# An earlier branch in the opening of a graph network and mixture-of-experts kernel, and means that are formed two slots later

## The chip, the cores and the metric

The kernel runs on one core of a Trainium2 chip. The metric is the device time in microseconds (us) of one execution, as the median of several runs. The engines are named as the profile names them: PE is TensorE (matrix products, with PEld its weight loads), DVE is VectorE, ACT is ScalarE, POOL is GpSimd, and SP is SyncE, which only starts transfers. A "q" behind an engine's name (DVEq) is that engine's sequencer, which fetches, waits and branches.

## The reference

There are 6250 nodes with 256 features and 100,000 edges with 96 features. Each edge belongs to the node whose number stands in `dst`, and `dst` is sorted. The computation, cut to what matters:

```python
h    = layernorm(x)
out1 = segment_sum(edge_attr, dst)          # 96 sums per node
cnt  = segment_sum(ones, dst)
out2 = where(cnt > 0, segment_max(edge_attr, dst), 0)
out3 = out1 / maximum(cnt, 1)               # the means
m    = concatenate([h, out1, out2, out3, u[0]])
x1   = x + h + relu(m @ W1 + b1) @ W2 + b2  # 608 -> 1024 -> 256
n    = layernorm(x1)
y    = n + (top 2 of 16 experts of n, weighted by a softmax)
out  = x1 + layernorm(y) * gamma + beta
```

## The kernel before

**Groups.** The nodes lie in 50 columns of 125 (`P`), and the columns in groups of up to four, taken from the highest node numbers down. Group 0 has two columns and group 1 has four. High nodes have few edges each, so groups 0 and 1 (`GW = 2`) are summed from *windows*: for each node the last 20 edges (`WE`) that end at its last edge are fetched and those of other nodes are masked out. All later groups take their sums and maxima from a stream over all edges, which runs on DVE beside the rest (`edge_stream`) and writes running sums to DRAM (`rows_d`).

**The opening.** Before any window can be fetched the kernel has to know where each node's edges lie. `block_starts` (L442 to L447) takes the first id of each block of 250 ids. `find_block` (ACT, L476) counts, for one column of nodes, how many blocks begin below each node. `take_blocks` turns this into a block number (DVE, L480 to L482) and fetches that block of ids for each of the 125 nodes (POOL, L485, an indirect transfer per column). `find_edge` (ACT, L492) counts in the block. `bounds` (DVE L502 and L503, PE L506 and L507) makes the place of each node's first and last edge. `index_windows` (DVE, L536 to L545) makes the window's address `win_i` and the mask `mk`, and `take_window` (POOL, L550) fetches the window, 125 x 1920 values per column.

**The check and the branch.** `check_order` (DVE, L258 to L260) and `check_fit` (DVE L266 to L268, PE L270, DVE L272 to L275) test that the ids are sorted and fit the layout, and leave a flag `misfit`. Every engine reads the flag (L1262) and branches (L1263): a body behind `tc.If`, which sums edges one by one, is run where the ids don't fit. With the given ids it isn't run, and each engine jumps over it.

**Statistics.** `stats_x` (DVE, L676 and L677), `root_x` (ACT, L682), `scale_x` (DVE, L688 to L690) and `norm_x` (ACT, L696) are the layer norm of a group's node features. `global_part` (PE L1212, DVE L1213) makes the part of the hidden layer's bias that comes from `u`. `loads_3` starts three small loads on SP.

**Windows.** For each column a window is cut twice over in two halves: `cut_window` (ACT, L558, ten rows of edges each) multiplies by the mask, for group 0 partly by DVE (L561); `sum_window` (PE, L581) adds the cut rows; `max_window` (DVE, L592, L571, L572) takes the masked maximum in the window's own buffer, so it has to wait until both cuts of the window are made; `add_window` and `mask_window` (DVE, L588 and L598) finish the sums; `mean_window` (ACT, L603 and L604) scales them to the means. Then `turn` transposes 128 features of a group at a time (PE L745, copied by ACT L746), `hidden` is the first layer (PE L756 and L761, ACT L763), and `output` the second (PE L769).

**What sets the order.** There are two stretches written by hand, ahead of the branch and behind it, each under `tc.manual_schedule()`. The second one ends with a planner: `at_slot(T, fn, ..., cost)` puts a step into a list with a due slot `T`; the list is sorted by slot and, within a slot, by the order of entry, and is then issued in that order. A group has twelve slots (`SLOTS`); a `cost` says how much DVE time a step takes from what the slot leaves for the edge stream. `mean_window` has no cost. Each engine runs its own list in order. The builder that turns this text into a program may carry single instructions ahead: in the program of before, the subtraction of `counts(0)` (L513), which the text has behind the branch, stands ahead of it on DVE, between L538 and L539.

Of the kernel before, what the change touches and what calls it, by code (L numbers as in the profile page):

```python
# [9 lines left out]
F32 = mybir.dt.float32  # L10
# [9 lines left out]
P = 125  # L20
PA = 80
RR = 8
GW = 2
# [4 lines left out]
JS = 3  # L28
# [6 lines left out]
SLOTS = 12  # L35
# [7 lines left out]
def kernel(  # L43
# [20 lines left out]
    E, EF = edge.shape  # L64
# [376 lines left out]
    def block_starts():  # L441
        nc.vector.tensor_copy(dsf, ids100[:, 0:E // 100].rearrange("p (q k) -> p q k", k=KB)[:, :, 0])  # L442
        nc.vector.tensor_tensor(dsx, ident[:100, None, :100].to_broadcast([100, QB, 100]),
                                dsf[:, :, None].to_broadcast([100, QB, 100]), op=OP.mult)
        ps_b = eps.tile([P, NBK], F32, name="ps")
        nc.tensor.matmul(ps_b, ones[:100, :P], dsx.rearrange("p q k -> p (q k)"), start=True, stop=True)
        nc.scalar.copy(b1r, ps_b)  # L447
# [22 lines left out]
    def node_cols(b):  # L470
        g0 = sum(IB[:b])
        return GRP[g0 + IB[b] - 1][0], GRP[g0][1]

    def find_block(t):
        junk = ix.tile([P, NBK], BF16, name="junk")
        nc.scalar.activation(junk, b1r, AF.Sign, scale=-1.0, bias=nhalf[:, t:t + 1], accum_out=acc1[:, t:t + 1])  # L476

    def take_blocks(a, z):
        cols = slice(a, z)
        nc.vector.tensor_scalar(blk_f[:, cols], acc1[:, cols], float(NBK), 0.5, op0=OP.add, op1=OP.mult)  # L480
        nc.vector.tensor_scalar(blk_f[:, cols], blk_f[:, cols], -1.0, 0.0, op0=OP.add, op1=OP.max)
        nc.vector.tensor_copy(blk_i[:, cols], blk_f[:, cols])  # L482
        for t in reversed(range(a, z)):
            gbs_[t] = ix.tile([P, KB], I32, name="gb", bufs=6)
            nc.gpsimd.indirect_dma_start(out=gbs_[t], out_offset=None, in_=dst_b,  # L485
                                         in_offset=IndirectOffsetOnAxis(ap=blk_i[:, t:t + 1], axis=0))
# [591 lines left out]
    def at_slot(T, fn, *a, cost=0.0):  # L1078
        tasks.append((T, len(tasks), fn, a, cost))
# [21 lines left out]
    for g, (a, z) in enumerate(GRP):  # L1101
        B, n = SLOTS * g, z - a
        if g:
            if g > 1:
                at_slot(max(0, B - 20), take_x, g)
                at_slot(B - 14, stats_x, g, 0, cost=1.2)
                at_slot(B - 13, stats_x, g, 1, cost=1.2)
            if g > 1:
                at_slot(B - 11, root_x, g)
                at_slot(B - 10, scale_x, g, cost=0.5)  # L1110
            at_slot(B - 9, norm_x, g)
            for i in range(n):
                if g >= GW:
                    late = 3 if g == GW else 0
                    at_slot(B - 10 + late + i // 2, take_edges, region[g], g, i)
                    at_slot(B - 9 + late + i // 2, take_carry, region[g], g, i)
                else:
                    for h in range(2):
                        at_slot(2 * i + h, cut_window, g, i, h * WE // 2, (h + 1) * WE // 2, None)
                        at_slot(2 * i + 1 + h, sum_half, g, i, h)  # L1120
                    at_slot(2 * i + 1, max_window, g, i, cost=4.7)
                    at_slot(2 * i + 2, add_window, g, i, cost=0.9)
                    at_slot(2 * i + 2, mask_window, g, i, cost=0.4)
                    at_slot(2 * i + 3, mean_window, g, i)
            at_slot(B - 7, keep_x, g)
            for k in range(DC):
                at_slot(B - 6 + k, turn, g, k)
            for i in range(n if g >= GW else 0):
                at_slot(B - (4 if g == GW else 6) + i // 2, join_edges, g, i, cost=0.6)
                at_slot(B - (4 if g == GW else 5) + i // 2, mask_edges, g, i)  # L1130
            for k in range(DC, KC + 1):
                at_slot(B - 3 + k - DC + (1 if g == GW and k < DC + 2 else 0), turn, g, k)
        for i in range(n):
            at_slot(B + HC + 1 + i, residual, g, i, cost=1.1)
        early = GS - n
        at_slot(B + SLOTS + 1 - early, root_b, g)
        at_slot(B + SLOTS + 2 - early, scale_b, g, cost=0.3)
        at_slot(B + SLOTS + 3, norm_b, g)
        for k in range(DC):
            at_slot(B + SLOTS + 4 + k, turn_b, g, k)  # L1140
        at_slot(B + SLOTS + 6, logits, g)
        at_slot(B + SLOTS + 7, choose, g, cost=2.2)
        at_slot(B + SLOTS + 8, rank, g, cost=1.3)
        at_slot(B + SLOTS + 9, rank_2, g)
        at_slot(B + SLOTS + 10, place, g, cost=1.5)
        for i in range(n):
            at_slot(B + SLOTS + 11 + i // 2, send, g, i)
# [16 lines left out]
    for b in range(GW, len(IB)):  # L1164

        a, z = node_cols(b)
# [59 lines left out]
    with tc.manual_schedule():  # L1226
        load_all_ids()
        loads_1()
        nc.gpsimd.memset(base[0], 0.0)
        loads_2()  # L1230
        more_constants()
        limits()
        nc.scalar.copy(gap, eps_t[0:1])
        nc.vector.memset(fill, 0.0)
        block_starts()
        for t in reversed(range(a, z)):
            find_block(t)
        take_blocks(a, z)
        for t in reversed(range(a1, z1)):
            find_block(t)  # L1240
        take_blocks(a1, z1)
        check_order()
        check_fit()
        global_part()
        stats_x(0, 0)
        for t in reversed(range(*node_cols(GW))):
            find_block(t)
        for t in reversed(range(a, z)):
            find_edge(t)
        bounds(0)  # L1250
        index_windows(0)
        for i in range(z - a):
            take_window(0, i, windows_of(rawp.tile([P, RR, JS, EF], F32, name="raw"), 1)[0])
        root_x(0)
        scale_x(0)
        norm_x(0)
        stats_x(1, 0)
        stats_x(1, 1)
        root_x(1)
        scale_x(1)  # L1260
        loads_3()
        bad_v = nc.values_load(misfit[0:1, 0:1])  # L1262
    with tc.If(bad_v != 0):  # L1263

# [39 lines left out]
        for t in range(NT - W0):  # L1304
            nc.vector.tensor_scalar(base[0][:, t, :], base[0][:, t, :], nw[:, t:t + 1], None, op0=OP.mult)
    with tc.manual_schedule():
        counts(0)
        for t in reversed(range(a1, z1)):
            find_edge(t)
        bounds(1)  # L1310
        index_windows(1)
        for h in range(2):
            for w in windows_of(rwp.tile([P, RR, JS, 2 * EF], F32, name="rw"), 2):
                take_window(1, len(G[1].get("win", [])), w)
        for k in range(DC):
            turn(0, k)
        for i in range(z - a):
            cut = (cut_w, cut_x)[i]
            cut_window_2(0, i, WE // 2, WE, cut)
            cut_window(0, i, 0, WE // 2, cut)  # L1320
            for half in range(2):
                sum_window(0, i, cut, half)
        for i in range(z - a):
            max_window(0, i)
            add_window(0, i)
            mask_window(0, i)
            mean_window(0, i)
        counts(1)
        nc.sync.dma_start(w2s, w2.rearrange("(k p) d -> p k d", p=128))
        for k in range(DC, KC + 1):  # L1330
            turn(0, k)
        cuts += [cut_x]
        for i in range(2):
            load_edges(i)
        for c in range(1, len(JR)):
            load_ids(c)
        keep_x(0)

        tasks.sort(key=lambda t: t[:2])
        T, credit = 0, SLOT  # L1340
        clock[0] = 0
        for slot, _, fn, args, cost in tasks:
            while slot > T:
                tell_pe()
                while credit > 0 and T >= SLOTS * (GW - 1) - 3:
                    cost_e = next(stream, None)
                    if cost_e is None:
                        break
                    credit -= cost_e
                g = min(T // SLOTS, NG - 1)  # L1350
                T, credit = T + 1, min(credit, 0.0) + SLOT * (GRP[g][1] - GRP[g][0]) / GS
                clock[0] = T
            if fn is take_edges:
                edges_until(args[0])
            fn(*args)
            credit -= cost
        for b in range(NA, NS):
            run_block(b, NS)
            if b % 4 == 0 and b // 4 - NA // 4 - 1 <= len(BATCH) // 2:
                load_x1()  # L1360
# [113 lines left out]
```

## Time and profile before

| | |
|---|---|
| median of 3 runs | 1451.49 us (1448.58 to 1451.82) |
| the profiled execution | 1458.22 us |
| its span, first to last instruction | 1456.4 us |
| busy: PE, DVE, ACT, POOL | 82%, 61%, 35%, 36% of the span |
| mean granted clock of PE | 0.924 |

| stretch, us | what runs | PE busy | DVE busy | ACT busy | POOL busy |
|---|---|---|---|---|---|
| 0 to 31 | opening, ahead of the branch | 6.79 | 15.94 | 14.53 | 15.04 |
| 31 to 51 | the branch, up to the first window | 2.20 | 4.96 | 1.67 | 2.33 |
| 51 to 70 | the windows of group 0 | 11.10 | 14.27 | 8.63 | 5.27 |
| 70 to 123 | hidden layer of group 0, windows of group 1 | 44.17 | 32.10 | 38.85 | 13.60 |
| 123 to 200 | hidden layer of group 1, the edge stream begins | 43.07 | 53.71 | 22.28 | 20.69 |

A row of the timeline gives start and length in us, the engine, the line of the kernel, the operation, what it writes and reads, its shape and how many such instructions were put together; in brackets is how long the engine was idle before it and what ended that. A row of the waits gives who waited for whom, the sum in us, how many times, and the longest. "issue" means that nothing in the profile explains the idle time.

### The profile page before, as it was taken

What the parts mean: (1) busy time and instruction counts of PE and PEld (TensorE: products, weight loads), DVE (VectorE), ACT (ScalarE), POOL (GpSimd) and SP (SyncE); (2) the same over time, 40 slices, a digit from 0 to 9 for tenths busy, and PEclk for the clock granted to TensorE, in tenths of its full rate; (3) what the DMA queues carried; (4) which work ended last, traced back from release to release, by engine and by line L of the source; (5) the groups of instructions that cost most, each with busy time, mean ns of one, the idle gap of its engine ahead of it and who ended that gap; (6) DMA issues with size and microseconds to landing.
All of it is one profiled execution on the core that took longest, in us unless ns stands there. A gap on an engine that the chain in (4) does not pass through costs nothing. (4 is left out here: it accounts for less than half of the span.)

```text
span 1456.4 us, 16537 instructions
## 1 busy us (share of the span) xinstructions
PE 1201.5 (82%) x4835; PEld 836.6 (57%) x4835; DVE 895.5 (61%) x2319; ACT 511.1 (35%) x1178; POOL 530.4 (36%) x611
## 2 busy tenths in 40 slices
PE   1488367969786869898877999898999999999683
PEld 1254143626444435655444566777888888888562
DVE  5467768868785969998596432344444454444277
ACT  4275234544345533442324342221221222122133
POOL 4232042573656553373342531324333332333100
PEclk9998688979987989999988999999999999999897
DMA  5664777686679897887878313556666887766296
GB/s 146 155 146 119 193 205 205 182 237 176 204 214 238 228 266 197 246 235 193 238 207 234 100 47 125 179 189 221 216 231 239 272 272 232 233 229 217 91 269 198
DMA packets 156310, 292.28 MB, mean 201 GB/s; under 512 B 31379, under 2 KB 95652, under 8 KB 148910
## 3 DMA queue, kind: packets, MB, share of 16 engines
q1 hardware_dynamic: 119870, 234.35, 54.5%
q0 software_dynamic: 36224, 56.33, 13.5%
q8 instruction: 42, 0.69, 0.2%
q14 instruction: 62, 0.51, 0.1%
q10 hardware_dynamic: 112, 0.41, 0.1%
HBM read 169.70 MB, written 123.21 MB: 201 GB/s over the span
## 5 line engine op out<-in xcount | busy, mean ns | idle before, releaser
L761 PE MATMUL acc<-inT,w1x 128*128 128x500 f32 (+1 forms) x832 | 377.2, 604 | 0.0
L761 PEld LDWEIGHTS acc<-inT,w1x 128*128 128x128 f32 x832 | 163.6, 204 | 182.1 <-issue 180.6
L1066 POOL DMA_INDIRECT y_d<-yb,to_i x114 | 133.1, 1168 | 294.3 <-ACT yb L1065 271.6
L1047 PE MATMUL acc<-xT,wt 128*128 128x256 f32 x912 | 222.7, 387 | 8.1 <-ACT hb L1053 6.4
L1060 PE MATMUL acc<-wt,hb 128*128 128x256 f32 x912 | 207.8, 380 | 6.4 <-DVE hb L1051 6.4
L874 POOL DMA_INDIRECT xg_d<-xr,pos_i x100 | 130.0, 1300 | 222.8 <-DVE xr L870 142.8
L769 PE MATMUL acc<-w2s,hT 128*125 128x256 f32 x800 | 194.5, 402 | 10.0 <-ACT hT L763 10.0
L1047 PEld LDWEIGHTS acc<-xT,wt 128*128 128x128 f32 x912 | 169.2, 191 | 39.9 <-ACT hb L1053 17.2
L1060 PEld LDWEIGHTS acc<-wt,hb 128*128 128x128 f32 x912 | 172.5, 190 | 32.3 <-DVE hb L1051 8.8
L769 PEld LDWEIGHTS acc<-w2s,hT 128*125 128x125 f32 x800 | 158.5, 202 | 36.9 <-ACT hT L763 10.4
L1065 ACT ACTIVATE yb<-yb,xb 128x256 f32<-128x256 f32 x114 | 51.8, 501 | 348.6 <-issue 300.6
L763 ACT ACTIVATE hT<-acc,c 128x500 f32<-128x500 f32 (+1 forms) x104 | 68.4, 657 | 210.8 <-PE acc L761 210.7
L1063 DVE TENSOR_TENSOR yb<-acc,xb 128x512 f32<-128x512 f32 x57 | 39.4, 691 | 163.1 <-PE acc L1060 163.1
L309 DVE TENSOR_TENSOR rw<-rw,keep 125x768 f32<-125x768 f32 x81 | 77.8, 961 | 83.1 <-DMA rows_d<-rw 83.1
L485 POOL DMA_INDIRECT gb<-in_dst_dram,blk_i x50 | 71.1, 1423 | 118.4 <-DVE blk_i L482 52.6
L1027 DVE COPY xT<-pT 128x512 f32<-128x512 f32 x57 | 39.3, 690 | 74.3 <-PE pT L1025 74.1
L313 DVE TENSOR_TENSOR rw<-rw,raw 125x768 f32<-125x768 f32 x88 | 83.7, 951 | 0.0
L312 DVE TENSOR_TENSOR rw<-rw,raw 125x768 f32<-125x768 f32 x88 | 83.5, 949 | 0.0
L310 DVE TENSOR_TENSOR rw<-rw,bar 125x768 f32<-125x768 f32 x81 | 82.0, 1013 | 0.0
L719 POOL DMA_INDIRECT cg<-carry_d,next_i x44 | 67.5, 1535 | 37.2 <-DMA carry_d<-ct 15.6
L712 POOL DMA_INDIRECT at<-rows_d,first_i x44 | 61.0, 1385 | 34.9 <-issue 18.5
L746 ACT COPY inT<-pT 128x500 f32<-128x500 f32 (+1 forms) x65 | 35.9, 552 | 105.8 <-PE pT L745 105.8
(294 smaller groups left out, 1510.9 us busy)
## 6 DMA issues: line engine op xcount, KB each, us to landing
wt<-in_wpack_dram SPq DMA_DIRECT2D x57, 1026.0 KB
rows_d<-rw SPq DMA_DIRECT2D x27, 1440.0 KB
rows_d<-rw SPq DMA_DIRECT2D x27, 810.0 KB
raw<-in_edge_dram SPq DMA_DIRECT2D x27, 720.0 KB
xb<-xg_d SPq DMA_DIRECT2D x57, 258.0 KB
raw<-in_edge_dram SPq DMA_DIRECT2D x27, 405.0 KB
eb<-in_eb_dram SPq DMA_DIRECT2D x57, 128.0 KB
rows_d<-rw SPq DMA_DIRECT2D x7, 960.0 KB
```

What stands on the lines that cost most here:

```text
L309: nc.vector.tensor_tensor(su, prev[0], keep[c][:, :, s + j, None].to_broadcast(bcast), op=OP.mult)
L310: nc.vector.tensor_tensor(mx, prev[1], bar[c][:, :, s + j, None].to_broadcast(bcast), op=OP.min)
L312: nc.vector.tensor_tensor(su, su, x_j, op=OP.add)
L313: nc.vector.tensor_tensor(mx, mx, x_j, op=OP.max)
L485: nc.gpsimd.indirect_dma_start(out=gbs_[t], out_offset=None, in_=dst_b, in_offset=IndirectOffsetOnAxis(ap=blk_i[:, t:t + 1], axis=0))
L761: nc.tensor.matmul(pH[:, :n * P], w1x[:, k, ms], inT[:, k, :n * P], start=False, stop=(k == KC - 1))
L763: nc.scalar.activation(h[:, :n * P], pH[:, :n * P], AF.Relu, bias=c1[:, m:m + 1])
L769: nc.tensor.matmul(pO, G[g]["hT"][m][:, i * P:(i + 1) * P], w2s[:, m, :], start=(m == 0), stop=(m == HC - 1))
L874: d = nc.gpsimd.indirect_dma_start(out=xg_d[:, :], out_offset=IndirectOffsetOnAxis(ap=G[g]["pos"][:, i, k:k + 1], axis=0), in_=G[g]["xr"][ ...
L1047: nc.tensor.matmul(pB[i][:, half, :], wt[:, k * FF + m * 128:k * FF + (m + 1) * 128], xT[:, k, :], start=(k == 0), stop=(k == DC - 1))
L1060: nc.tensor.matmul(pY[:, h, :], hb[:, m, h * 128:(h + 1) * 128], wt[:, W2O + m * D:W2O + (m + 1) * D], start=(m == order[0]), stop=(m == o ...
L1066: d = nc.gpsimd.indirect_dma_start(out=y_d[:, :], out_offset=IndirectOffsetOnAxis(ap=BL[b]["to"][:, h:h + 1], axis=0), in_=yb[:, h, :], in ...
```

## The change

Three things move, and nothing is added or taken out.

1. `check_order` and `check_fit` move up between the steps of the block search, and the branch follows right behind the fetch of the id blocks of group 1.
2. What stood between the check and the branch now stands behind it: the global part, the statistics of groups 0 and 1, the edge places and the window fetches of group 0, the block search of the first later block of groups (`node_cols(GW)`), and `loads_3`. Among them `counts(0)` and the edge places of group 1 are now placed ahead of the norm of group 0, and group 1's window fetches ahead of its statistics.
3. `mean_window` of group 1 has the slot `2 * i + 5`, at most 10, in place of `2 * i + 3`, for each of its columns `i` from 0 to 3.

```diff
-                    at_slot(2 * i + 3, mean_window, g, i)
+                    at_slot(min(2 * i + 5, SLOTS - 2), mean_window, g, i)
...
         block_starts()
+        check_order()
         for t in reversed(range(a, z)):
             find_block(t)
         take_blocks(a, z)
         for t in reversed(range(a1, z1)):
             find_block(t)
+        check_fit()
         take_blocks(a1, z1)
-        check_order()
-        check_fit()
-        global_part()
-        stats_x(0, 0)
-        for t in reversed(range(*node_cols(GW))):
-            find_block(t)
-        for t in reversed(range(a, z)):
-            find_edge(t)
-        bounds(0)
-        index_windows(0)
-        for i in range(z - a):
-            take_window(0, i, windows_of(rawp.tile([P, RR, JS, EF], F32, name="raw"), 1)[0])
-        root_x(0)
-        scale_x(0)
-        norm_x(0)
-        stats_x(1, 0)
-        stats_x(1, 1)
-        root_x(1)
-        scale_x(1)
-        loads_3()
         bad_v = nc.values_load(misfit[0:1, 0:1])
     with tc.If(bad_v != 0):
...
     with tc.manual_schedule():
+        global_part()
+        stats_x(0, 0)
+        for t in reversed(range(a, z)):
+            find_edge(t)
+        bounds(0)
+        index_windows(0)
+        for i in range(z - a):
+            take_window(0, i, windows_of(rawp.tile([P, RR, JS, EF], F32, name="raw"), 1)[0])
+        root_x(0)
         counts(0)
         for t in reversed(range(a1, z1)):
             find_edge(t)
+        scale_x(0)
+        norm_x(0)
         bounds(1)
         index_windows(1)
         for h in range(2):
             for w in windows_of(rwp.tile([P, RR, JS, 2 * EF], F32, name="rw"), 2):
                 take_window(1, len(G[1].get("win", [])), w)
+        stats_x(1, 0)
+        stats_x(1, 1)
+        root_x(1)
+        scale_x(1)
+        loads_3()
+        for t in reversed(range(*node_cols(GW))):
+            find_block(t)
         for k in range(DC):
             turn(0, k)
```

In the built program, the branch stands on DVE behind 57 listed instructions where it stood behind 74, on ACT behind 16 where it stood behind 26, and on POOL behind 25 where it stood behind 27. On PE and SP the same instructions stand ahead of it as before.

## The prediction

> **What bounds the kernel now.** I read the waits of the first 72 us first, then VectorE's timeline there, the rows of the branch, the transfers of the windows, and last the waits of 70 to 123 us, where group 1 is summed. The rest of the page (PE 82% busy, 1384 of the 1456 us behind 72 us) runs in an order that this change leaves as it is.
>
> The waits of 0 to 72 us:
> ```profile
> PEld pg L506 <- DVE rp L503: 20.8, 2, 19.2
> ...
> ACT inT L746 <- PE pT L745: 18.7, 4, 16.4
> POOL rw L550 <- DVE m L540: 17.4, 1, 17.4
> ...
> DVE cnt L514 <- DVEq L1263: 8.7, 1, 8.7
> ...
> DVE nw L519 <- issue: 4.5, 1, 4.5
> ```
> PE, ACT and POOL stand 16 to 19 us, ACT by way of PE, for VectorE, and VectorE stands 8.7 us at the branch (L1263) and, four instructions later, 4.5 us for nothing that has a record. Its timeline:
> ```profile
> 33.67 0.16 DVE L690 TENSOR_SCALAR rs<-rsa 125x4 f32<-125x4 f32 x1
> 42.49 0.22 DVE L514 SCALAR_TENSOR_TENSOR cnt<-cnt,nf,cnt_f 125x2 f32<-125x2 f32 x1 [8.65 <-DVEq L1263]
> ...
> 47.65 0.23 DVE L519 TENSOR_SCALAR nw<-ne_n,nf 125x2 f32<-125x2 f32 x1 [4.46 <-issue]
> ...
> 51.60 1.20 DVE L561 TENSOR_TENSOR xr<-raw,mk 125x960 f32<-125x960 f32 x1
> 53.95 2.16 DVE L592 TENSOR_TENSOR raw<-raw,mk 125x1920 f32<-125x1920 f32 x1 [1.15 <-ACT w2s L558]
> ```
> From L592 at 53.95 the two windows of group 0 run back to back on VectorE to 66.0; PE's first hidden product (L756) starts at 69.26. The branch rows, engine by engine:
> ```profile
> L1263 DVEq EVENT_SEMAPHORE  x2: 21/21/21, 42.1 to 42.2; - x2
> L1263 SPq COMPARE_BRANCH  x1: 45/45/45, 23.7 to 23.7; - x1
> ...
> L1263 ACTq COMPARE_BRANCH  x1: 45/45/45, 33.6 to 33.6; - x1
> L1263 DVEq COMPARE_BRANCH  x1: 72/72/72, 34.2 to 34.2; - x1
> L1263 ACTq EVENT_SEMAPHORE  x1: 17/17/17, 41.2 to 41.2; - x1
> ```
> The compare takes under 0.1 us; what costs is the way to the next instruction: 7.9 us on VectorE, 7.6 on ACT, 2.8 on SP (23.7 to its first semaphore at 26.5). PE (28.7 to 29.2) and POOL (30.3 to 30.8) pass in 0.5.
>
> The windows of group 0, then the waits of 70 to 123 us:
> ```profile
> DMA to landing us min/median/max: 14.1/15.0/16.0
> ```
> ```profile
> DVE rw L592 <- ACT xr L558: 22.6, 4, 13.1
> ...
> ACT at L603 <- DVE at L598: 10.1, 4, 3.8
> ```
> Group 1's four windows run in a ring: ACT cuts a window (L558), VectorE reduces it (L592 to L598, 6.0 us), ACT forms the mean (L603, L604). ACT stands at each mean for VectorE with the next window's second cut queued behind it; VectorE then stands for that cut.
>
> **The change, part by part.** I go by the order in which the built programs list each engine's instructions. It is not the order of the text: the builder carries work back over the branch. In the new one the edge places of group 0 up to L542 still stand ahead of the branch on VectorE, with their products on PE, group 0's two finds and its root on ACT, and SP's three loads. What does pass behind it: on VectorE 17 instructions (L544, L545, L513, both L688 to L690, group 1's eight statistics); on ACT the finds of group 1 (L492), four finds of blocks (L476), L696 and the second root; on POOL the two window gathers of group 0.
>
> *Ahead of the branch.* The three passes over the ids (L258 to L260, 3.6 us from 16.07) start behind L443, at 8.4, and end at 12.0, inside VectorE's 3.9 us wait for ACT: free. Group 0's block places stay at 12.3 to 12.9. The reduction (2.23), L267, L268, the product on PE and L272 follow to 16.1, where they ended at 22.9; PE's L1212 takes 16.2 to 19.8 (3.57). Group 1's block places straddle L1213, which waits for it, so its four gathers start at 20.8 instead of 16.45 and, at 1.51 each, end at 26.5. Group 0's finds stay at 21.6 (its gathers don't move), so L502 comes at 21.6 (was 27.73), and through PE (1.26 us from L503 to L536) the window places at 23.6 (was 29.7).
>
> *POOL.* It reaches its branch with the gathers queued, jumps in about 0.5, and issues the windows when its gathers end: 26.8 and 28.3 (was 30.0 and 31.5). Landing after 14.1 and 16.0: 40.9 and 44.3.
>
> *VectorE behind the branch.* It reads the flag at 23.9 and branches at 24.4. Here a rule of the Trainium skill speaks against the change. The row has 7.9 us, then 4.5. "Runtime: NRT & Kernel Launch", section Instruction fetch mechanics, says that a taken branch to a page not held must fetch it by DMA before it goes on. The same dead body is jumped over, so the fetch stays, and more work now lies behind it. If its price is fixed, VectorE resumes at 32.3, group 1's places come at 35.1 to 38 and, with a second 4.5, statistics and L690 end near 45.5, past the windows; the two L561 follow and L592 comes at 47.8, a gain of 6.1. But the row isn't fixed: SP paid 2.8 in the same branch at 23.7, when only the small block gathers moved, ACT and VectorE 7.6 and 7.9 at 34 us while the windows moved. At 24.4 the traffic is SP's, so I take 2.8 (ends 0.5 and 7.9): VectorE at 27.2, ACT at 26.4. ACT's four finds wait for group 1's last gather (25.3 + 5 = 30.3; L485's landings took 3.8 to 5.6) and end at 31.1; L502 to L545 run 31.2 to 34.0 (2.84 from 47.78); statistics 2.3, root and L688 to L690 1.0: ready at 37.3. That is 7 us ahead of the second window, which hides all that was moved here, ACT's four L476 (3.0 us) too; without that cover they would cost up to 3.3 us.
>
> *Sum of the opening.* The second L561 at 44.4, L592(0) at 45.6 (ACT's cut of the first window ends at 43.8): 53.95 − 45.6 = **8.4 us**. Bounds: POOL could need a fetch of 7.9 (windows at 29.1: gain 6), or a window could land at the slowest seen of this line, 29.5 (both L561 end at 59, a loss of 5); landings sooner than before give up to 10.
>
> *Means two slots later.* In the time frame of before: ACT ends L696 at 85.6 and cuts window 1 at once, to 88.35; bias and relu 0.45, cut 2a to 91.5, relu, mean 0 (0.6), cut 2b 92.5 to 95.25 (was 96.09 to 98.84); L704, relu, cut 3a, copy, find, relu to 102.3, mean 1, cut 3b 102.9 to 105.65 (was 109.62 to 112.37). VectorE starts the last window at 105.7 instead of 112.40 and ends at 111.7; POOL's L706 (2.4) now falls on it as it fell on L598 (2.52 for 0.42 at 106.5), so 111.7 to 113.7, I take 112.7: 5.7 sooner than 118.4. Against it, mean 3 now stands behind a copy and two finds (2.0 us) ahead of PE's transposes: −1.2. **4.5 us**, bounds 2 (the last mean hurts fully, POOL collides twice) and 6.5.
>
> *Behind that* every engine's order is the old one, and loads are issued by what they wait for, so the shift is carried to the end: 12.9. Profiled span 1456.4 − 12.9 = 1443.5, with the 1.8 us around it (1458.22 − 1456.4) 1445.3. The profiled execution lies 6.7 over the median 1451.49; subtracting the same from the median gives **1439**.
>
> **Rivals.** *Only the opening or only part of it:* group 1's ring is limited by VectorE or PE instead (PE has 44 us of 53 busy there), or a fetch on POOL takes 2 us of the first: 1451.5 − 8.4 = 1443, or 6 + 0: 1445. For it: that share of PE. Against: the idle of ACT at L603 is 10.1 us and the next cut stands right behind. *Absorbed:* 123 to 200 us is bound by VectorE's edge stream and its transfers (DVE busy 54 of 77, PE 43), and what comes sooner waits there: 1449 to 1452. Against: that stream starts from the same program slots, and its loads wait for buffers that these windows free. *The clock takes it back:*
> ```profile
> 70.00:123.00 53.00, 44.17 (x164) 27.94 (x156) 32.10 (x54) 38.85 (x129) 13.60 (x9) 0.92 0.71 176
> 123.00:200.00 77.00, 43.07 (x127) 21.92 (x128) 53.71 (x130) 22.28 (x50) 20.69 (x15) 0.74 0.60 165
> ```
> (after the stretch: PE, PEld, DVE, ACT, POOL busy, then the granted clock, DMA). PE is granted 0.74 right after group 1. PE with fewer pauses could be cut back earlier and for longer. PE is busy 174 us from 70 to 300; a mean clock lower by 7% there costs 12.9 us and cancels all; at 10% the kernel is 4 to 5 us slower, 1456. Against: PE is only 56% busy in the 0.74 stretch, so load alone doesn't set it.
>
> **How the numbers follow.** Both gains (1434 to 1443): 0.60. One of them or part (1441 to 1447): 0.22. Absorbed, within 0.3% (about 4.4 us, what a measurement can tell from no change): 0.10. The clock, slower: 0.08. Faster is the first two, 0.82. The range 1433 to 1448 leaves out the slower case, most of the absorbed one and a little below: 0.18. The likeliest case alone has 1434 to 1443.
>
> **What would show it.** After: misfit written near 16 us; VectorE's branch near 24 with a wait of about 3, and no 4.5 us gap; window gathers at 27 and 28; a new wait of VectorE's L561 for the window, about 7 us; L592 first at 46; L603's waits in group 1 mostly gone; the first long product of group 1's hidden layer about 13 us sooner than 126.7. It is wrong if VectorE or ACT pays 8 us or more at the branch and again behind it, if the windows land later than 45, or if a 13 us lead at 126 is smaller at 300.

## The result, and the profile after

| | before | changed |
|---|---|---|
| median of 19 runs each, side by side | 1451.82 us | 1443.29 us |
| ratio, with 95% interval | | 0.9929 (0.9912 to 0.9946) |
| the profiled execution, and its span | 1458.22, 1456.4 us | 1443.29, 1441.3 us |
| mean granted clock of PE | 0.924 | 0.925 |

The ratio is that of the fast runs (one of the changed kernel's 19, at 1457.13 us, was slow and is left out) and stands for 10.3 us less, 7.8 to 12.8; the two medians alone lie 8.5 us apart. The forecast was 1439, range 1433 to 1448. In the changed kernel the branch stands at L1245.

The waits of the first 72 us of the changed kernel; the columns are the sum in us, how many, and the longest:
```profile
DVE w2s L561 <- DMA raw<-in_edge_dram,win_i: 4.6, 1, 4.6
DVE mk L544 <- DVEq L1245: 4.2, 1, 4.2
POOL rw L550 <- DVE m L540: 4.2, 1, 4.2
...
DVE c L1213 <- PE ps L1212: 3.3, 1, 3.3
DVE xr L561 <- DMA raw<-in_edge_dram,win_i: 3.2, 1, 3.2
...
DVE ne_n L515 <- issue: 1.6, 1, 1.6
```
VectorE's stand at the branch went from 8.7 to 4.2, the nameless gap behind it from 4.5 to 1.6, and POOL waits 4.2 for group 1's places where it waited 17.4. New are the waits of L561 for the windows, 7.8 in all: what lies behind the branch ends ahead of the data, and the landing of the windows now sets the start.

The timeline of the same kernel, the same steps as shown of before:
```profile
19.17 0.17 DVE L1213 TENSOR_TENSOR c<-ps,b1c 128x8 f32<-128x8 f32 x1 [3.29 <-PE ps L1212]
...
26.16 1.21 POOL L550 DMA_INDIRECT raw<-in_edge_dram,win_i  x1 [0.30 <-issue]
...
27.59 0.18 DVE L544 TENSOR_SCALAR mk<-mk 125x40 f32<-125x40 f32 x1 [4.16 <-DVEq L1245]
27.68 1.21 POOL L550 DMA_INDIRECT raw<-in_edge_dram,win_i  x1 [0.30 <-issue]
...
41.10 1.16 DVE L561 TENSOR_TENSOR w2s<-raw,mk 125x960 f32<-125x960 f32 x1 [4.59 <-DMA raw<-in_edge_dram,win_i]
...
45.49 1.16 DVE L561 TENSOR_TENSOR xr<-raw,mk 125x960 f32<-125x960 f32 x1 [3.22 <-DMA raw<-in_edge_dram,win_i]
...
46.56 2.15 DVE L592 TENSOR_TENSOR raw<-raw,mk 125x1920 f32<-125x1920 f32 x1
```
L592 starts at 46.56 where it started at 53.95: 7.4 us sooner. The branch rows of the changed kernel:
```profile
L1245 DVEq EVENT_SEMAPHORE  x2: 21/21/21, 27.4 to 27.5; - x2
L1245 SPq COMPARE_BRANCH  x1: 45/45/45, 18.0 to 18.0; - x1
...
L1245 ACTq COMPARE_BRANCH  x1: 45/45/45, 21.1 to 21.1; - x1
...
L1245 DVEq COMPARE_BRANCH  x1: 67/67/67, 23.9 to 23.9; - x1
L1245 ACTq EVENT_SEMAPHORE  x1: 17/17/17, 24.0 to 24.0; - x1
```
From the compare to the first semaphore VectorE needs 3.5 us (before 7.9) and ACT 2.9 (before 7.6).

Group 1's windows, first in the waits of 60 to 112 us and then in the timeline of the changed kernel:
```profile
DVE rw L592 <- ACT xr L558: 19.0, 4, 12.8
...
PE pT L745 <- ACT at L603: 0.9, 1, 0.9
```
```profile
96.68 2.40 POOL L706 TENSOR_TENSOR xt<-xt,b2b 125x1024 f32<-125x1024 f32 x1
...
97.22 3.90 DVE L592 TENSOR_TENSOR rw<-rw,mk 125x1920 f32<-125x1920 f32 x1 [3.56 <-ACT xr L558]
```
The waits of L603 for L598, 10.1 us, have left the ring, and the last window starts at 97.22 instead of 112.40: 15.2 us sooner, of which 7.7 were there at the ring's first window (72.39 instead of 80.07). L706 falls on it and stretches L592 from 2.16 to 3.90, so its end (L598) is 13.4 sooner. The first relu of group 1's hidden layer (L763) comes at 118.6 instead of 131.0: 12.4. Two rows of the kernel before, then one of the changed kernel:
```profile
112.40 2.16 DVE L592 TENSOR_TENSOR rw<-rw,mk 125x1920 f32<-125x1920 f32 x1 [3.36 <-ACT xr L558]
...
131.03 0.68 ACT L763 ACTIVATE hT<-acc,c 128x500 f32<-128x500 f32 x1 [7.22 <-PE acc L761]
```
```profile
118.60 0.68 ACT L763 ACTIVATE hT<-acc,c 128x500 f32<-128x500 f32 x1 [7.48 <-PE acc L761]
```

PE's clock, in the stretches that answer to those of before (columns as there):
```profile
62.00:111.00 49.00, 42.67 (x168) 28.71 (x168) 30.68 (x57) 40.16 (x132) 13.87 (x10) 0.92 0.64 160
111.00:187.00 76.00, 41.27 (x123) 20.39 (x124) 51.53 (x121) 21.05 (x49) 18.63 (x14) 0.75 0.61 167
```
0.92 and 0.75, where it was 0.92 and 0.74.

### The profile page after: what moved, and what is told of

Its sections match the earlier page's. It is cut to its first block, busy times and chain, and to the rows that moved or that the text cites. A ratio compares the mean times of both kernels' runs of the same rounds, so it can differ in the third digit from the quotient of the medians.

```text
span 1441.3 us, 16536 instructions
## 1 busy us (share of the span) xinstructions
PE 1193.9 (83%) x4835; PEld 833.1 (58%) x4835; DVE 892.9 (62%) x2319; ACT 511.2 (35%) x1178; POOL 530.9 (37%) x611
## 5 line engine op out<-in xcount | busy, mean ns | idle before, releaser
L769 PE MATMUL acc<-w2s,hT 128*125 128x256 f32 x800 | 190.0, 395 | 11.5 <-ACT hT L763 11.5
L1047 PEld LDWEIGHTS acc<-xT,wt 128*128 128x128 f32 x912 | 168.1, 190 | 39.2 <-ACT hb L1053 15.7
L769 PEld LDWEIGHTS acc<-w2s,hT 128*125 128x125 f32 x800 | 155.2, 198 | 36.5 <-ACT hT L763 11.9
L763 ACT ACTIVATE hT<-acc,c 128x500 f32<-128x500 f32 (+1 forms) x104 | 68.4, 658 | 208.5 <-PE acc L761 206.3
L485 POOL DMA_INDIRECT gb<-in_dst_dram,blk_i x50 | 69.2, 1383 | 115.8 <-DVE blk_i L482 54.2
L806 PE MATMUL pT<-ident,xr 125*128 125x125 f32 x100 | 23.3, 320 | 53.8 <-ACT xr L797 44.6
```

What stands on the lines that cost most here:

```text
L769: nc.tensor.matmul(pO, G[g]["hT"][m][:, i * P:(i + 1) * P], w2s[:, m, :], start=(m == 0), stop=(m == HC - 1))
L1047: nc.tensor.matmul(pB[i][:, half, :], wt[:, k * FF + m * 128:k * FF + (m + 1) * 128], xT[:, k, :], start=(k == 0), stop=(k == DC - 1))
```

## The experiments

In what follows "lead" is by how much an instruction starts sooner than in the profiled execution of before. The leads up to 131 us come out within 1.6 us of each other whenever the changed kernel is profiled: at the last window's L592 15.2, 13.8 and 14.1 in three profiles. Behind it they wander by several us from one execution to the next; the same kernel had profiled spans of 1441.3, 1444.4 and 1428.4. The kernel before has one profile, whose own chance is in every lead: from 300 to 390 us all 13 profiles gain 1.8 to 9.7 us on it, whatever the kernel. So the opening and the ring are read from the traces, and the end from the ratios alone.

### The two halves

The first: the changed kernel with the old slot of the means.
```diff
-                    at_slot(min(2 * i + 5, SLOTS - 2), mean_window, g, i)
+                    at_slot(2 * i + 3, mean_window, g, i)
```


> The check, the branch and the opening as in the changed kernel, the means in their old slots. Theory (two independent gains): the first masked maximum (L592) of group 0 comes at 46.6 us as in the changed kernel (before: 53.95), group 1's four windows take as long as before (first L592 to last L598 about 38 us), the lead at group 1's hidden layer is about 7 us and is carried to the end: 0.995 of before. Rival (the opening's lead is lost behind it, the whole gain is the means'): within 0.1% of before.

Measured: 0.9963 (0.9944 to 0.9982), 5.4 us. The lead is 7.5 at the first L592, 8.0 at all four L592 of group 1 and at its last L598, 6.5 at the hidden layer.

The second: the kernel before with the new slot.
```diff
-                    at_slot(2 * i + 3, mean_window, g, i)
+                    at_slot(min(2 * i + 5, SLOTS - 2), mean_window, g, i)
```


> The kernel before with the means two slots later and nothing else. Theory: the opening is that of before (L592 at 54), ACT's waits at L603 in group 1 (10.1 us) fall to under 1 us, first L592 to last L598 of group 1 takes 32 us where it took 38, and the lead at the hidden layer is 5 us: 0.9965 of before. Rival (the ring is set by PE or VectorE themselves): no more than 1 us, 0.999 to 1.000.

Measured: 0.9974 (0.9950 to 0.9997), 3.8 us. The lead is 0.8 at the first L592, 0.4, 1.6, 4.0 and 7.9 at the four of group 1, 6.2 at the last L598, 5.9 at the hidden layer. The branch costs what it cost before: 8.1 and then 3.9 us on VectorE.

The two gains arise in different places, and each shows alone, that of the means at the end only just (0.9997). At the hidden layer 6.5 + 5.9 = 12.4, the lead in the changed kernel's first profile; that it fits to the tenth is luck, since its other two profiles have 10.8 and 12.2, and 0.4 of the 5.9 were there at the ring's first window, ahead of anything the means change. At the end 5.4 + 3.8 = 9.2, which the changed kernel's 7.8 to 12.8 holds. Neither needs the other.

### The check alone, with the branch where it was

The kernel before with `check_order` and `check_fit` in their new places and all else ahead of the branch:
```diff
         block_starts()
+        check_order()
...
+        check_fit()
         take_blocks(a1, z1)
-        check_order()
-        check_fit()
```


> The kernel before with the check moved up as in the changed kernel, but with all the work of groups 0 and 1 left ahead of the branch, old means. It asks what the branch's place adds to the check's. If the price of the jump depends on what moves: the windows are fetched at 23 to 25 us, VectorE branches near 28 with them in flight, pays about 8 us and then again 4 to 5, and L592 comes at 47: a lead of 6.5 to 7, 0.9955. If the price is about 3 us wherever the branch stands: VectorE is through by 33 and L592 waits for the windows only, 43 to 44: a lead of 10, 0.993. If the branch's place is what the change gains by: a lead under 3.

Measured: 0.9958 (0.9938 to 0.9978), 6.1 us. Its timeline:
```profile
23.66 1.21 POOL L550 DMA_INDIRECT raw<-in_edge_dram,win_i  x1 [1.04 <-DVE mk L542]
...
38.75 0.22 DVE L514 SCALAR_TENSOR_TENSOR cnt<-cnt,nf,cnt_f 125x2 f32<-125x2 f32 x1 [8.91 <-DVEq L1263]
...
42.12 0.23 DVE L519 TENSOR_SCALAR nw<-ne_n,nf 125x2 f32<-125x2 f32 x1 [2.67 <-issue]
...
48.42 2.16 DVE L592 TENSOR_TENSOR raw<-raw,mk 125x1920 f32<-125x1920 f32 x1 [1.15 <-ACT w2s L558]
```
The windows are on their way at 23.7, yet L592 begins at 48.42: VectorE branches at 30.2, stands 8.9 us at the branch and 2.7 behind it, and both L561 stand behind that. So the early check brings 5.5 of the 7.5 us of the opening. The place of the branch, with the new order behind it, brings the other 2 (1.0 to 2.0, taking the five profiles with the changed kernel's opening, 46.4 to 47.5), and not by removing the jump: an earlier jump meets less traffic, and what it delays ends ahead of the data. At the end this run and the first can't be told apart.

### What sets the price of the jump

The kernel before, with the fetches of group 0's windows moved behind those of group 1, so that no window is under way when VectorE branches at 33.9, practically where it branches in the kernel before (34.2):
```diff
-        for i in range(z - a):
-            take_window(0, i, windows_of(rawp.tile([P, RR, JS, EF], F32, name="raw"), 1)[0])
         root_x(0)
...
                 take_window(1, len(G[1].get("win", [])), w)
+        for i in range(z - a):
+            take_window(0, i, windows_of(rawp.tile([P, RR, JS, EF], F32, name="raw"), 1)[0])
```


> The kernel before with the two window fetches of group 0 issued behind group 1's four, so that nothing moves when VectorE and ACT branch at 34 us. It measures the price of the jump alone and is slower as a whole (group 0's windows land behind four others, 15 to 25 us later). If the traffic of the windows makes the price: VectorE's wait at the branch 3 to 4 us where it was 8.65, the second wait under 2 us where it was 4.5. If the jump's price is that of VectorE and ACT as such: 8 and 4.5 again.

Measured, in one run: 1477.09 us. Its waits of 0 to 90 us:
```profile
DVE cnt L514 <- DVEq L1261: 3.9, 1, 3.9
...
DVE nw L519 <- issue: 1.3, 1, 1.3
```
At the same moment, over the same body, the branch costs 3.9 + 1.3 us instead of 8.7 + 4.5. The traffic of the windows makes the difference.

The profile's list of transfers shows what the jump waits for. Packets that bring instructions stand there as a kind of their own, 8 KB each in queue q14; a row has the queue and kind, then packets, MB and their share of the 16 DMA engines' time. In the kernel before, from 34 to 39 us, there is none, only rows of the windows:
```profile
q0 software_dynamic: 115, 0.88, 64.0%
```
From 39 to 40.4 us two come, at 39.2 and 39.8:
```profile
q14 instruction: 2, 0.02, 5.0%
```
In the run with the late windows two come from 34.4 to 35.6 us, at 34.5 and 34.9, and nothing else moves:
```profile
q14 instruction: 2, 0.02, 4.5%
```
The packets don't name their engine. ACT branches first, so the second of each pair is taken for VectorE's: it moves 5.6 us behind the compare in the kernel before (34.2 to 39.8) and 1.0 us here (33.9 to 34.9), and VectorE goes on 2.3 and 2.0 us behind its start. In the changed kernel the packet that lies as far ahead of VectorE's next step (2.0 us) moves at 25.3, 1.5 us behind the compare. The second stall ends 1.8 to 1.9 us behind another such packet (45.8, 37.6 and 28.0). In these profiles a packet takes 0.3 to 0.8 us; what differs is how long it stands back beside the windows' rows.

With this the price in the changed kernel (4.2 + 1.6) is explained: its windows are issued at 26.2 and 27.7, behind the compare at 23.9, and their first row moves at 28.1. It is a narrow escape: the second packet moves at 27.98, 0.1 us ahead of that row (0.0 and 0.4 us in the other two profiles). In two later runs, with the global part later and with all three edits, it moves 2.2 and 4.7 us behind the first row, and the second stall is 2.5 and 4.8 us.

The run as a whole is slower because the windows come 18 us later: L592 starts 20.7 us late, and the lag is 20.3 at the hidden layer and 18.9 at the end of the profiled spans.

### Steps beyond the change

The changed kernel's VectorE waits 3.3 us for L1212 at L1213, with group 1's block places behind it, whose four gathers stand ahead of the windows on POOL. The next run moves `global_part()` behind group 1's window fetches, to take that wait away:
```diff
-        global_part()
         stats_x(0, 0)
...
                 take_window(1, len(G[1].get("win", [])), w)
+        global_part()
```


> The changed kernel with the global part (L1212, L1213) placed behind group 1's window fetches, so that group 1's block places no longer wait for it and its four gathers leave POOL sooner. Theory (the opening now ends with the landing of group 0's windows): the windows are fetched at 23.2 and 24.7 us instead of 26.2 and 27.7, L592 of group 0 comes at 43.6 instead of 46.6, and 3 us are carried to the end: 0.991 of before against 0.993 for the changed kernel. Rival (VectorE or ACT behind the branch is the bound, or the jump gets dear again because the windows now move under it): L592 stays within 1 us of 46.6.

Measured: 0.9944 (0.9922 to 0.9967), and the lead at L592 only 4.4: a miss. The timeline of its first 14 us:
```profile
8.10 0.43 DVE L676 BATCH_NORM_STATS2 bsa<-xt 125x6 f32<-125x256 f32 x1 [7.15 <-DMA xt<-in_x_dram]
...
12.69 0.10 DVE L442 CAST dsf<-rw 100x4 f32<-100x4 int32 x1
```
With the global part no longer ahead of them, the statistics of group 0 were carried by the builder to the head of VectorE's list, where they wait 7.1 us for the node features. L442, which opens the search, comes at 12.7 instead of 7.1. Counted from L442, the windows are issued after 15.5 us, where the changed kernel needs 19.0 (26.16 − 7.11): the wait on L1213 did go, and more was lost ahead of it. At the end of the opening ACT's first cut holds L592 for another 0.7 us, since its norm (L696) has waited 7.1 us for the late L1212. I had first read this run as group 1's sooner gathers getting in the way of group 0's; a later run tells the two apart.

Beside it, the ring: in the changed kernel L706 falls on the last L592, so group 1's features are kept (L704, L706) behind the windows:
```diff
-            at_slot(B - 7, keep_x, g)
+            at_slot(B - 2 if g == 1 else B - 7, keep_x, g)
```


> The changed kernel with group 1's keep_x (ACT L704, POOL L706) moved from five slots ahead, to slot 10 of group 0, where ACT stands idle. Theory (the last window's reduction is late by ACT's cut behind L704, 2.06 us, and by POOL's L706 on top of it, 1.7 us): the last L592 takes 2.2 us where it took 3.9, the last L598 of group 1 ends 3 to 4 us sooner, and the lead at the hidden layer grows by about 3 us: 0.991. Rival (PE's own work, which waits less and less, is what ends the ring): under 1 us.

Measured: 0.9923 (0.9902 to 0.9944). The last L598 is 15.9 ahead, where the changed kernel profiled beside it has 12.1; at the hidden layer 12.5 against 10.8. More than half is lost on the way there, since L704 now stands ahead of a copy (L746) that PE waits for. At the end the two can't be told apart.

Both edits, with the last mean one slot earlier:
```diff
-                    at_slot(min(2 * i + 5, SLOTS - 2), mean_window, g, i)
-            at_slot(B - 7, keep_x, g)
+                    at_slot(min(2 * i + 5, SLOTS - 3), mean_window, g, i)
+            at_slot(B - 2 if g == 1 else B - 7, keep_x, g)
...
-        global_part()
...
+        global_part()
```


> Both of these edits and the last mean one slot sooner (slot 9, ahead of the copy and the two finds that it stands behind in the changed kernel). If the gains are independent: 3 + 3 + 1 us more than the changed kernel, a lead of 19 to 20 us over before at group 1's hidden layer, 0.988 of before. If they share one bound: 0.990 or above.

Measured: 0.9944 (0.9922 to 0.9966), far from the 0.988 of independent gains; it lies where one shared bound was expected (0.990 or above), but for another reason. The opening's lead is 1.3. L442 comes at 13.1, as in the run with the global part later (12.7), and the second stall at the branch, 4.8 us where that run had 2.5, costs most of the rest: L1213 and ACT's L696, which wait for the late L1212, come 3.1 us later than there, and so does L592. The ring brings the lead to 10.7.

And the changed kernel again, beside these three:

> The changed kernel itself once more, on the chip of the three others, so that they can be compared: 0.993 of before, L592 of group 0 at 46.6 us, the jump at 3.5 us on VectorE and 3 on ACT, the last L592 of group 1 at 3.9 us.

Measured: 0.9927 (0.9902 to 0.9952); the lead 6.5 at the first L592, 12.1 at the last L598, 10.8 at the hidden layer. L442 started at 7.8 here, 0.7 later than in the first profile of the changed kernel.

### Holding the statistics back

The global part later, and group 0's statistics behind its window fetches, so that they can't be carried to the head:
```diff
-        global_part()
-        stats_x(0, 0)
...
             take_window(0, i, windows_of(rawp.tile([P, RR, JS, EF], F32, name="raw"), 1)[0])
+        stats_x(0, 0)
         root_x(0)
...
                 take_window(1, len(G[1].get("win", [])), w)
+        global_part()
```


> The changed kernel with the global part moved behind group 1's window fetches, as in the run with the global part later, and with the statistics of group 0 (L676, L677) moved behind group 0's window fetches. In the run with the global part later the builder carried those statistics to the head of VectorE's list, where they waited 7.1 us for the node features and pushed everything behind them; the two theories are that this alone made that run's opening late, or that group 1's earlier gathers get in the way of group 0's. If the first holds: no wait of VectorE for L1213, group 1's gathers at 16.4 to 21 us, windows of group 0 issued at 23.2 and 24.7 (26.2 and 27.7 in the changed kernel), L592 first at 43.5 to 44.5 (46.6 to 47.4 there), and the ratio to the kernel before 0.990 to 0.993, some 2 us under the changed kernel beside it. If the second holds: group 0's finds come 2 us or more later than in the changed kernel, and L592 first comes no sooner than 46.6.

Measured: 0.9921 (0.9892 to 0.9951). Group 1's gathers start at 16.6, group 0's finds at 19.9 (19.8 in the changed kernel), and the windows are issued at 23.5 and 25.0. So the gathers are not in the way, and it was the statistics. Yet L592 starts at 47.53, no sooner than in the changed kernel:
```profile
37.95 1.09 ACT L696 ACTIVATE xn<-xt,nba,rsa 125x256 f32<-125x256 f32 x2 [4.99 <-PE ps L1212]
...
44.74 2.76 ACT L558 ACTIVATE w2s<-raw,mk 125x96 f32<-125x96 f32 x10
...
47.53 2.16 DVE L592 TENSOR_TENSOR raw<-raw,mk 125x1920 f32<-125x1920 f32 x1 [4.33 <-ACT w2s L558]
```
`norm_x` writes the tile named `xn`, of which there is one, and `w1u`, which L1212 reads, lies in it. With L1212 late, L696 waits 5.0 us, the four finds of L476 (3.0 us) follow it, and ACT comes to the first cut at 44.74, though both L561 had read the windows at 41.0 and 42.1 without a wait. This is the price of those four finds once their cover is gone.

The same with both edits of the ring:
```diff
-                    at_slot(min(2 * i + 5, SLOTS - 2), mean_window, g, i)
-            at_slot(B - 7, keep_x, g)
+                    at_slot(min(2 * i + 5, SLOTS - 3), mean_window, g, i)
+            at_slot(B - 2 if g == 1 else B - 7, keep_x, g)
```


> The run with group 0's statistics held back, and in addition the mean of the last window one slot earlier and the keeping of group 1's features (L704, L706) behind the windows instead of among them. If gains in the opening and in the ring add up and are carried on: L592 last about 3 us sooner than in the run with the statistics held back alone, and the ratio 0.988 to 0.991. If what lies behind 131 us limits the end, no clear difference to the changed kernel beside it, ratio 0.991 to 0.994.

Measured: 0.9918 (0.9893 to 0.9942). The lead is 6.5 at the first L592, 16.4 at the last, 14.4 at the hidden layer.

> The changed kernel itself, beside the two others: ratio 0.991 to 0.9945, L592 first at 46.5 to 47.5.

Measured: 0.9923 (0.9895 to 0.9951), the lead 6.8 at the first L592, 14.1 at the last, 12.2 at the hidden layer. All three are alike at the end, which the second expectation for the run with the ring allowed.

The last run leaves the product L1212 where it is and moves only its addition behind the window fetches, with the statistics behind it and both edits of the ring:
```diff
-        nc.vector.tensor_add(c1, ps_u, b1c)
+        return lambda: nc.vector.tensor_add(c1, ps_u, b1c)
...
-        global_part()
-        stats_x(0, 0)
+        add_global = global_part()
...
             take_window(0, i, windows_of(rawp.tile([P, RR, JS, EF], F32, name="raw"), 1)[0])
+        add_global(); stats_x(0, 0)
         root_x(0)
```


> The changed kernel with only the addition of the global part (L1213) moved from ahead of group 1's block places to behind group 0's window fetches, its product L1212 left where it is on PE, group 0's statistics behind that addition, and both edits of the ring (the last mean one slot earlier, L704 and L706 behind the windows). In the run with the statistics held back the windows were issued 2.7 us sooner and yet L592 began no sooner, since ACT's norm (L696) waited 5.0 us for L1212 to free the tile it shares with w1u, and the four L476 behind it ended at 43.3. If that wait was the reason: no wait of L696 for L1212, ACT's L476 end near 39 to 40, its first cut of group 0 starts at 41 to 42 (44.7 there, 41.1 in the changed kernel), L592 first at 44 to 45.5 (47.5 there, 46.6 to 47.4 in the changed kernel), last near 94 to 96, and the ratio 0.988 to 0.991. If the landing of the windows holds it instead: VectorE's L561 waits for the windows and L592 first stays at 46.5 or later.

Measured: 0.9901 (0.9871 to 0.9931), 1440.57 us against 1454.59 beside it. Its timeline:
```profile
24.66 1.21 POOL L550 DMA_INDIRECT raw<-in_edge_dram,win_i  x1 [0.30 <-issue]
...
31.14 1.08 ACT L696 ACTIVATE xn<-xt,nba,rsa 125x256 f32<-125x256 f32 x2
...
40.74 2.78 ACT L558 ACTIVATE w2s<-raw,mk 125x96 f32<-125x96 f32 x10
...
42.45 1.16 DVE L561 TENSOR_TENSOR xr<-raw,mk 125x960 f32<-125x960 f32 x1 [3.35 <-DMA raw<-in_edge_dram,win_i]
...
43.55 2.16 DVE L592 TENSOR_TENSOR raw<-raw,mk 125x1920 f32<-125x1920 f32 x1
```
L696 doesn't wait, the cut starts at 40.74, and L592 at 43.55, a lead of 10.4; the last L592 leads by 19.5 and the hidden layer by 17.0. The shared tile was the reason, and with it out of the way the landing of the second window binds again. This is the best of the kernels run, 14.4 us under the one before by its ratio, but its interval overlaps that of the changed kernel, so that it beats the changed kernel is likely and not shown.

## Why the prediction was right, step by step

| step | predicted | measured |
|---|---|---|
| misfit written (L273) | 16 | 15.54 |
| group 1's gathers start | 20.8 | 20.10 |
| windows of group 0 issued | 26.8, 28.3 | 26.16, 27.68 |
| VectorE branches; resumes | 24.4; 27.2 | 23.9; 27.4 |
| VectorE ready for the windows | 37.3 | 36.5 |
| windows landed | 40.9, 44.3 | 41.1, 45.5 |
| L592 first: gain | 8.4 | 7.4, 6.5, 6.8 in three profiles |
| end of group 1's last window: gain in the ring | 5.7 | 13.4 − 7.7 = 5.7 |
| last mean ahead of PE's transposes | −1.2 | −0.9 and −1.2 (PE, PEld) |
| both, at group 1's hidden layer | 12.9 | 12.4, 10.8, 12.2 |
| the end | 12.9 | 10.3 (7.8 to 12.8), by ratio |

**The mechanism** was the one forecast: the early check lets the windows go 3.8 us sooner, the jump is cheap because no window moves yet, and what was moved behind it ends ahead of the data. With the early check alone, up to 2 us of the opening would be missing.

**The price of the jump** was where the sum depended on a choice. "Runtime: NRT & Kernel Launch", Instruction fetch mechanics, in the Trainium skill says that a taken branch to a page not held waits for its fetch. The rows agree: instruction packets move between the compare and the first step behind it, and again at the second stall, four instructions on. The fetch is not what costs, but its wait beside the windows' rows (5.6 us of the 7.9, against 1.5 of the 3.5). A fixed price of 7.9 + 4.5 would have given 6.1 us in the opening, by the prediction's own working, and the measured 6.5 to 7.4 lie between that and 8.4; the rows of the branch tell the two apart, not the gain. The choice of 2.8, read from SP's jump, was nearer: 3.5 on VectorE, and 2.9 on ACT. There was some luck in it: SP's own jump took 5.5 in the changed kernel. The gap behind the jump did not vanish, as the prediction expected, but shrank to 1.6 us, by a margin of 0.1 us ahead of the windows' first row, and the wait for the windows hides it.

**The mis-sized term** is the landing of the second window. The prediction took 16.0 us from issue to landing, from the kernel before. In the three profiles of the changed kernel it is 17.8 (27.68 to 45.49), 18.0 and 18.2, and 17.4 and 17.8 in two more runs with the same opening. In the changed kernel's first profile POOL issued it 0.6 us sooner than predicted, 0.5 of that since L442 happened to start at 7.1 instead of 7.6, and it took 1.8 us longer: 8.4 + 0.6 − 1.8 = 7.2, near the 7.4 read. Counted from L442, all three profiles have a gain of 6.5 to 6.9. In the kernel before, group 1's four windows are issued some 20 us behind group 0's; in the changed one at 33.0 to 37.6, while the second window is still landing. That they slow it down is the likely cause. In the changed kernel the DMA engines' share (the last column but one) rises to all that there is when group 1's rows begin:
```profile
30.00:35.00 5.00, 1.52 (x6) 1.13 (x6) 3.53 (x22) 1.09 (x2) 1.66 (x2) 1.00 0.62 175
36.00:46.00 10.00, 4.09 (x7) 1.78 (x8) 2.09 (x5) 6.69 (x23) 2.40 (x2) 1.00 1.02 225
```
and in the run with all three edits, which issues group 1's windows 10.4 us behind the second window instead of 5.4, that one landed after 14.4 us. But with 7.7 us, in the run with the global part later, and 8.9 us, in the last run, it took 18.0 and 17.8, and no run moves this alone, so the cause is not shown.

**The ring** was right in its mechanism, and to the tenth by luck, for two errors of 0.7 to 0.8 us cancel: the last window starts 7.5 us sooner within the ring (15.2 − 7.7) where 6.7 was forecast, and the collision with L706 costs 1.74 us (3.90 − 2.16), where up to 2 was allowed and 1 taken. The run that moves L706 away, where L592 takes 2.16 again, shows that the collision is the reason.

**One reading** of the prediction was too narrow: L485's landings in the kernel before took 3.8 to 7.1 us, not 3.8 to 5.6, since the three earliest of them were left out. The last one, taken as 5 us, was 3.9, and nothing hung on it.

**The end.** The lead at 131 us, some 11.8 us in the mean of three profiles, lies inside the interval of the end (7.8 to 12.8); the 12.9 of the forecast lies just outside it. A rigid carry to the end is not refuted, and not confirmed to better than 2.5 us.

**Its signs of being wrong.** VectorE and ACT paid less than 8 us at the branch. But the second window landed later than 45, at 45.5 (46.4 and 46.0 in the other two profiles), which is the mis-sized term above; and the lead at 300 us was smaller than at 131, 11.6, 10.7 and 9.4 where it was 12.4, 10.8 and 12.2. How much of that is loss and how much the wandering of single executions stays open.

**The rivals.** Only part of it, 1443 to 1445: the median of 1443.29 alone could not tell it from both gains; the two halves refute it, since each shows. Absorbed behind 123 us, within 4.4 us of no change: refuted by the interval, though a loss of a few us is not. The clock: the mean is 0.925 against 0.924, and 0.75 against 0.74 in the stretch that was feared for.

## What to carry to other kernels

Ask of a stall at a branch what else is moving on the DMA queues then: the same jump cost 3.9 + 1.3 us or 8.7 + 4.5 us, and moving a large transfer across the branch in the program's order changes it. Ask also by what margin the jump escapes it: 0.0 to 0.4 us in the changed kernel. Work behind a branch is free only as far as something else ends later; list each engine's queue up to that point, and look for tiles that two steps share, because a step that is made later holds whoever reuses its tile. After each edit of the order, look at the head of every engine's list: freeing one wait let the builder put another, 7.1 us long, at the very front.

## What was unexpected of the hardware

- SP's jump took 5.5 us (compare at 18.0, first semaphore at 23.5) in the changed kernel, where it took 2.8 in before: the sooner jump was the dearer one there. It costs nothing, since SP has only loads behind it. The likely reason is traffic again: in the changed kernel the loads of the hardware queue (q1) move until 22.9, and the first instruction packet at 21.7; in before those loads have ended at 22.8, SP compares at 23.7, and the packet moves at 24.7. In all 14 profiles the jump takes 5.4 to 5.5 us where SP compares ahead of the end of those loads (nine) and 2.5 to 2.8 behind it (five). No run tests this alone.
- The jump's price is split in two: a first stall at the branch and a second one, in eleven of the 14 profiles exactly four instructions later on VectorE, and both follow the traffic (4.2 + 1.6, 3.9 + 1.3, 8.9 + 2.7, 8.7 + 4.5 us). In the three runs with the statistics held back there is no second stall on VectorE; why stays open.
- In the last run the compare on VectorE came at 23.9, 0.8 us behind the first window's issue, and the wait was still only 3.8 us; in the run with the check alone it came 6.6 us behind it and the wait was 8.9. The windows' first row moves some 1.9 us behind the issue (25.1 and 25.6): not the issue, but the data under way make the jump dear.
